# New step times for two list-scheduled stages, a pause step before the page scatters, and the further pages' lists built in pieces

## The chip, the cores and the metric

One core of one Trainium2 chip runs the whole program in one launch. The core has a matrix engine (PE, TensorE), a vector engine (DVE), a scalar engine (ACT), a general engine (POOL, GpSimd) and a sync engine (SP), each with its own queue of instructions that it works off in order; transfers go through DMA queues that SP and POOL fill. The metric is the device time of one execution in microseconds (us); less is better.

## The reference

The input x has 4 batches of 256 tokens with 256 numbers each. Four sublayers follow one another, each as `x = x + layernorm(sublayer(layernorm(x)))`:

```python
# 1 attention over chunks of 32 tokens: 16 query heads, 4 key heads, 128 numbers a head
scores = einsum("bld,bcd->blc", qr, lmk) / sqrt(32)      # token against chunk landmarks
rw  = softmax(scores of the chunks that lie before the token)
att = softmax(q @ k over the 32 tokens of each chunk) * rw[chunk]
out = (att @ v) @ w_o.T + residual

# 2 mixture of experts: 32 experts, each token goes to its best 4
top, idx = top_k(x @ gate_w.T + gate_b, 4); w = softmax(top)
for the rows of one expert:
    gate = minimum(x @ w_gate + b_gate, 7); up = clip(x @ w_up + b_up, -7, 7)
    y = ((up + 1) * gate * sigmoid(1.702 * gate)) @ w_down + b_down
out = sum of the 4 y of a token, weighted by w

# 3 gated scan along the tokens
lam = sigmoid(x @ W.T + b);  s = lam * s + (1 - lam) * x

# 4 gated network with int8 weights, 1024 inner units
out = ((silu((x @ w_gate) * s_gate) * ((x @ w_up) * s_up)) @ w_down) * s_down
```

The 1024 tokens make 8 tiles of 128 tokens, two to a batch. 1024 tokens times 4 choices are 4096 rows for the experts.

## The kernel before

**The planner.** Two stages, attention with routing and the last layer (sublayers 3 and 4), are not written in the order in which they run. Their code is cut into steps, and `Plan` (L49 to L109) decides the order. A step has an engine letter (T is PE, V DVE, A ACT, P POOL, S SP, J a step of no time that only gives buffers back, others are arrivals of data), a cost in us, a list of steps that it comes after, buffers that it takes and gives, and a lead. `run` works backwards first: a step's rank is its lead or, if longer, the longest chain of costs behind it, with a fixed HOP of 0.12 us between two steps. Then it plays the engines forward in pretended time: each engine that is free takes the ready step of the highest rank whose buffers are free, and its code is written out then. So costs and hops do not run on the chip; they set the order in which the code of the steps is emitted. The dependencies on the chip are made from the tiles that the code touches. The framework that builds the program decides the order of the transfers and instructions of each engine again from there, so what runs may differ from the order of the text.

**Attention (the `aplan`, L311 to L997).** `batch(b)` (L572) adds the steps of one batch: statistics and a transposed copy of x, landmark scores and the chunk weights (`hidden`, `shares`, `spread`, `place`, `copy_rw`), keys and values (`keys`, `turn_k`, `values`), queries for each of four key heads (`queries` L821 with four matmuls of 128x512 named pq, `square_sums` L764 named jq, `norm_q` through `power` L336 on POOL named rq, `scale_q` named qn, `turn_q` named pqT), then for each key head the softmax over three pieces of scores: `stage1` on DVE, `less` on POOL (L874), `exps` on ACT, `sums` on DVE, `times` on POOL, `back` on DVE, and `weigh` on PE. The projection (`project` L968, matmuls wo of 128x256, eight to a step) makes the two tiles of a batch from four key heads each. A batch's steps start with the lead `(B - 1 - b) * LEAD`, with LEAD 22, so that earlier batches go first. Five buffers named att hold the weighed values of a key head, used in a fixed rotation.

**Routing (`routing` L400 to L563)** follows each projected tile: its layernorm (rmva, rve, rrsa), residual, the normed tile xn, which goes to DRAM as xn_dram (L440), the gate's matmul, the choice of four experts (`choose`), each row's rank within its expert (`ranks`, `slots`), the lists of who sits where on the pages (`listed`, `sum_lists` L517), and `places`, which makes rowi (L530), the four row numbers of each token. An expert has pages of 128 rows each. Then four scatters per tile (`scatter_token` L244, an indirect DMA issued by POOL) put the tile's xn rows into x_pages in DRAM. The scatters need the zero fill of x_pages to have landed (`ld_zero`). Tiles 0 to 5 add their four scatters right behind `places`, each behind the one before. Tile 6's scatters are held until tile 7's roots are done; tile 7's are issued in `pages`, behind the gathers of the first pages.

`front_ends` collects the steps that read the attention's input weights and xT. When all of them are through, `middle` (L988) frees that memory and loads the weights of experts 4 to 19 there (SP, the loads at L995).

**The pages (`pages` L1201).** 32 first pages and 16 further ones are worked off in pairs, so pg is 0, 2, and so on up to 46. For each pair: `page_fetch` (L1097) brings the rows, by gathers through POOL for the first 8 pages (L1119, index gi), by SP from x_pages for the others (L1100 first, L1110 further pages); `page_in` transposes them (px, pxT); `page_up` (L1145) multiplies with the gate and up weights (pg L1155), bounds the two halves on DVE (g L1160, u L1162), and makes h; `page_down` transposes h (ph, hT), multiplies (po L1184), and POOL scatters the result o into y_dram (L1191). `pages` fetches four pairs ahead, and calls `hook(pg)` once a pair behind `page_up` and the `page_down` of the pair before.

**The further pages' lists (`more_pages` L1228).** Which expert has more than 128 rows is known only after routing. `hook(0)` calls `more_pages`, which makes all of it at one go: the counts (ptot), how many further pages each expert has (more), their running ends (end, base), for each further page its expert (ex, from a comparison cmp of 128x1024 and a sum) and its place in x_pages (hot, again 128x1024, a product and a sum, place), then exi and placei, which SP reads as values to address weights and rows (`weights` L1087 with the value read L1092, `page_fetch` L1110), sel2, and then the row lists of the further pages: at2 and pq (L1283), slot (L1300, four operations), pick2 (L1307), ent2 (L1316, four), 32 matmuls into plist2 (L1324), and si for the scatters of the results. All of this is DVE work but the matmuls.

**The last layer (L1374 to L1651)** is a second `Plan`: weighting of the y_dram rows (mix), layernorms (lst, rss), gate, scan and the int8 network, with its products in pairs of high and low parts (fh, fl).

## Time and profile before

Three timed runs took 574.9, 576.89 and 577.91 us; the median is 576.89. The profiled execution took 573.4 us itself, and the span that the profile covers is 571.6.

| | profiled execution |
|---|---|
| own time, span | 573.4 us, 571.6 us |
| PE busy | 455.6 us, 80% |
| PE weight load | 308.6 us, 54% |
| DVE busy | 357.1 us, 62% |
| ACT busy | 237.7 us, 42% |
| POOL busy | 309.8 us, 54% |
| mean granted PE clock | 0.919 |
| moved by DMA | 80.68 MB |

A page of the profile begins with the busy time of each engine, its share of the span and its number of instructions. Rows of digits follow, one for each engine, with the busy share in tenths of 40 equal slices of the span; PEclk is the clock that PE was granted. A group line names the source line, engine, operation, result and operands, the count, the busy time and the mean in ns, and behind the second bar the engine's idle time just before such instructions with what ended most of it. The windows view gives the same for chosen stretches of the span: start and end, length, then busy time of PE, PE's weight load, DVE, ACT and POOL with the number of instructions in brackets, PE's clock, the share of time that the DMA engines worked, and GB/s. The timeline view lists instructions in order of time: start, duration, engine, line, operation, result and operands, size, and in square brackets the idle time before with what ended it.

The stages lie at these times: start and first loads 0 to 20 us; attention 20 to 315, of which the zero fill of x_pages shares the transfers until about 127; the last tiles' routing 315 to 341; pages 341 to 452; the landing of the last scatters 452 to 463; the last layer 463 to 571.6.

### The profile page before, as it was taken

The numbers are of one execution on the slowest core, as the hardware profiler recorded it, in microseconds if no ns is written. First come the engines' busy times: TensorE is split into PE (matmuls) and PEld (weight loads), VectorE is DVE, ScalarE is ACT, GpSimd is POOL, SyncE is SP. The second block draws the span as 40 slices with busy tenths as digits, with TensorE's granted clock in tenths as the row PEclk, the third lists the DMA queues.
The fourth block names the chain that finished last, engine by engine and source line by source line (L and its number), as shares of the span: only waits on it lengthen the run. The fifth ranks groups of instructions, "written<-read, shape, count | busy, mean of one in ns | idle before, by whom it ended". The sixth has DMA issues, their size and how long they took to land. (4 is left out here: it accounts for less than half of the span.)

```text
span 571.6 us, 7166 instructions
## 1 busy us (share of the span) xinstructions
PE 455.6 (80%) x1965; PEld 308.6 (54%) x1965; DVE 357.1 (62%) x1096; ACT 237.7 (42%) x760; POOL 309.8 (54%) x434
## 2 busy tenths in 40 slices
PE   1879988997959989948999336899999559689980
PEld 0334545754535735526768224677777347467850
DVE  3359985779736868939785673945644316863442
ACT  3556654244424345433331012234943105675541
POOL 7467674544674645676554473164554516766441
PEclk9999999999979998978999657899999969799996
DMA  8999999930010000010381563323857252000001
GB/s 257 361 387 365 349 349 347 336 129 2 20 55 1 11 10 0 20 55 29 120 303 56 177 246 122 98 92 124 306 208 253 83 200 96 1 1 0 10 29 37
DMA packets 59805, 80.68 MB, mean 141 GB/s; under 512 B 5684, under 2 KB 48682, under 8 KB 59760
## 3 DMA queue, kind: packets, MB, share of 16 engines
q1 hardware_dynamic: 54896, 70.33, 36.4%
q0 software_dynamic: 4576, 9.70, 5.0%
q10 hardware_dynamic: 288, 0.15, 0.2%
q8 instruction: 17, 0.28, 0.2%
q14 instruction: 28, 0.23, 0.1%
HBM read 37.16 MB, written 45.09 MB: 144 GB/s over the span
## 5 line engine op out<-in xcount | busy, mean ns | idle before, releaser
L821 PE MATMUL pq<-w_q,xT 128*128 128x512 f32 x128 | 64.6, 629 | 18.3 <-DVE lists L517 6.4
L968 PE MATMUL wo<-w_o,att 128*128 128x256 f32 x256 | 62.4, 387 | 1.2 <-DVE h L981 1.2
L968 PEld LDWEIGHTS wo<-w_o,att 128*128 128x128 f32 x256 | 48.1, 193 | 13.7 <-issue 5.1
L1191 POOL DMA_INDIRECT y_dram<-o,sia x32 | 32.0, 999 | 43.2 <-ACT o L1188 36.8
L821 PEld LDWEIGHTS pq<-w_q,xT 128*128 128x128 f32 x128 | 24.2, 198 | 41.3 <-issue 21.0
L336 POOL TENSOR_TENSOR rq<-ssq,mhalf 128x4 f32<-128x4 f32 x32 | 32.8, 1025 | 24.6 <-DVE ssq L830 18.4
L764 ACT ACTIVATE jq<-pq 128x128 f32<-128x128 f32 x128 | 33.4, 277 | 27.3 <-PE pq L821 26.4
L244 POOL DMA_INDIRECT x_pages<-rxn,rowi x32 | 31.8, 992 | 20.8 <-issue 7.2
L1155 PE MATMUL pg<-wexp,pxT 128*128 128x256 f32 x128 | 38.7, 418 | 4.0 <-ACT pxT L1142 3.8
L1160 DVE TENSOR_SCALAR g<-pg 128x256 f32<-128x256 f32 x24 | 10.1, 423 | 46.0 <-PE pg L1155 29.2
L836 DVE TENSOR_TENSOR qn<-pq,rq 128x512 f32<-128x512 f32 x32 | 21.7, 679 | 16.5 <-POOL rq L336 16.5
L1155 PEld LDWEIGHTS pg<-wexp,pxT 128*128 128x128 f32 x128 | 24.0, 211 | 10.3 <-ACT pxT L1142 4.0
L1572 POOL TENSOR_TENSOR fl<-f,fh 128x512 fp32r<-128x512 f32 x15 | 19.4, 1291 | 15.6 <-ACT fh L1568 15.6
L1467 PE MATMUL y<-yk,mix 128*128 128x256 f32 x64 | 17.9, 432 | 11.5 <-DMA yk<-y_dram 11.0
L844 PE MATMUL pqT<-ident,qn 128*128 128x128 f32 x128 | 20.7, 283 | 7.9 <-ACT qT L852 7.5
L764 ACT ACTIVATION_READ_ACCUMULATOR jq<-pq 128x1 f32 x128 | 26.6, 208 | 0.0
L1188 ACT COPY o<-po 128x512 f32<-128x512 f32 x24 | 14.1, 585 | 24.9 <-PE po L1184 20.4
L844 PEld LDWEIGHTS pqT<-ident,qn 128*128 128x128 f32 x128 | 15.7, 145 | 16.1 <-ACT qT L852 9.1
L1191 POOL DMA_INDIRECT y_dram<-o,sib x16 | 15.7, 984 | 15.3 <-ACT o L1188 12.6
L852 ACT COPY qT<-pqT 128x512 f32<-128x512 f32 x32 | 18.8, 587 | 8.6 <-PE pqT L844 8.6
L1467 PEld LDWEIGHTS y<-yk,mix 128*128 128x128 f32 x64 | 13.4, 218 | 15.1 <-issue 11.4
L1164 ACT ACTIVATE sg<-g 128x256 f32<-128x256 f32 x24 | 10.0, 417 | 26.4 <-DVE g L1160 24.3
(741 smaller groups left out, 1308.0 us busy)
## 6 DMA issues: line engine op xcount, KB each, us to landing
x_pages<-zeros SPq DMA_DIRECT2D x1, 31744.0 KB
wexp<-in_wcat SPq DMA_DIRECT2D x32, 384.0 KB
wov<-in_wcat SPq DMA_DIRECT2D x16, 384.0 KB
yk<-y_dram SPq DMA_DIRECT2D x8, 512.0 KB
xg<-x_pages SPq DMA_DIRECT2D x12, 256.0 KB
w_q<-in_wqT SPq DMA_DIRECT2D x4, 512.0 KB
w_o<-in_woT SPq DMA_DIRECT2D x2, 1024.0 KB
xg<-x_pages SPq DMA_DIRECT2D x16, 128.0 KB
```

What stands on the lines that cost most here:

```text
L244: nc.gpsimd.indirect_dma_start(out=x_views[i * TOPK + k], out_offset=IndirectOffsetOnAxis(ap=rowi[:, k : k + 1], axis=0), in_=xn, in_offse ...
L336: eng.tensor_tensor(dst, src, mhalf[:p, 0:1].to_broadcast([p, n]), ALU.pow)
L764: nc.scalar.activation(junk[:, 0:HD], src[:, ts(j, HD)], AF.Square, accum_out=dst[:, j : j + 1])
L821: nc.tensor.matmul(ps, keep[f"xT{b}"][:, k, ts(i, P)], wq[:, k, ts(kv, 512)], start=(k == 0), stop=(k == KD - 1))
L836: nc.vector.tensor_tensor(buf(p1, "qn", [P, G, HD], f"qn{n}"), keep[f"pq{n}"].rearrange("p (h d) -> p h d", h=G), rq[:, i, ts(kv, G)].unsq ...
L844: nc.tensor.transpose(ps[:, ts(j, P)], keep[f"qn{n}"][:, j, :], ident)
L852: nc.scalar.copy(keep[f"qT{b}{kv}"][:, :, ts(i, P)], keep[f"pqT{n}"].rearrange("p (h n) -> p h n", h=G))
L968: nc.tensor.matmul(keep[f"wo{b}{i}"][:, 0:D], keep[f"att{b}{kv}"][:, j, ts(i, P)], wo[:, kv * G + j, :], start=(kv == 0 and j == 0), stop= ...
L1155: nc.tensor.matmul(ps[:, j, :], xT[:, j, k, :], ws[j][:, ts(k, 2 * I)], start=False, stop=(k == KD - 1),)
L1191: nc.gpsimd.indirect_dma_start(out=y_views[pg + j], out_offset=IndirectOffsetOnAxis(ap=scl[:, q : q + 1], axis=0), in_=o[:, j, :], in_offs ...
L1467: nc.tensor.matmul(ps, mix[:, i * TOPK + k, :], keep[f"yk{i}"][:, k, :], start=(k == 0), stop=(k == TOPK - 1),)
L1572: eng.tensor_tensor(buf("fl", [P, HALF], f"fl{n}{o}", F32R), keep[f"f{n}{o}"], keep[f"fh{n}{o}"].bitcast(F32), ALU.subtract,)
```

## The change

The planner gets a hop for each engine, and keeps, for a step, the latest of its forerunners' ready times rather than that of the last one to end:

```diff
-    def __init__(self):
+    def __init__(self, hops=None):
+
+        self.hops = hops or {}
...
-                rank[a] = max(rank[a], rank[i] + self.HOP)
+                rank[a] = max(rank[a], rank[i] + hop(self.steps[a][0]))
...
                 for j in then[i]:
                     waits[j] -= 1
+                    when[j] = max(when[j], now + cost + hop(eng))
                     if not waits[j]:
-                        heapq.heappush(events, (now + cost + self.HOP, 1, j))
+                        heapq.heappush(events, (when[j], 1, j))
```

Both plans use it, LEAD is smaller, and some 100 costs are rewritten, nearly all to less. Some of them:

```diff
-        aplan = Plan()
+        aplan = Plan({"T": 0.25, "V": 0.15, "A": 0.18, "P": 0.1, "J": 0.0})
...
-        LEAD = 22.0
+        LEAD = 19.0
...
-            a = add("V", 0.65, [a], stats_a)
+            a = add("V", 0.42, [a], stats_a)
...
-            lg = add("T", 0.8, [xT], logits, take=["mm"])
+            lg = add("T", 0.4, [xT], logits, take=["mm"])
...
-                    qt = add("T", 1.8, [xT, ld_wq[kv], turns.get("q")], queries, take=["mm"])
+                    qt = add("T", 1.73, [xT, ld_wq[kv], turns.get("q")], queries, take=["mm"])
...
-                    a = add("A", 1.9, [qt], lambda i=i, kv=kv, n=n: square_sums(
+                    a = add("A", 1.0, [qt], lambda i=i, kv=kv, n=n: square_sums(
...
-                    a = add("P", 1.05 * cols_ / 448, [a], less)
+                    a = add("P", 0.92 * cols_ / 448, [a], less)
...
-        plan = Plan()
+        plan = Plan({"T": 0.25, "V": 0.15, "A": 0.18, "P": 0.1, "S": 1.3})
...
-            a = plan.add("T", 2.0, ready_u, gate, take=["g"])
+            a = plan.add("T", 1.73, ready_u, gate, take=["g"])
```

In routing, the scatters of tiles 0 to 5 each come behind a step of 2.4 us on a pretended engine W, which emits nothing, and tile 6's `places` has a larger lead:

```diff
-            pl = add("V", 0.85, [sl, xn], places, lead=5.0)
+            pl = add("V", 0.5, [sl, xn], places, lead=12.0 if i == TT - 2 else 5.0)
...
-                    at = aplan.add("P", 1.35, [at, ld_zero, *more], put,
+                    if i < TT - 2:
+
+                        at = aplan.add("W", 2.4, [at, ld_zero])
+                    at = aplan.add("P", 1.3, [at, ld_zero, *more], put,
                                    give=["xn"] if k == TOPK - 1 else [])
```

In attention, `place` and `turn_k` join `front_ends`; the att buffers come from a list that the projection of a batch's second tile fills again; and that projection's step for a key head comes behind the first tile's step for the same head:

```diff
+            front_ends.append(a)
             rws = add("V", 0.1, [a], copy_rw, give=["mm"])
...
-                            keep[f"att{b}{kv}"] = atts[(b * HKV + kv) % NATT]
+                            keep[f"att{b}{kv}"] = atts.pop(0)
...
+            first_tile = []
             for i in range(2):
...
+                        if i == 1:
+                            atts.append(keep[f"att{b}{kv}"])
...
+                    if i == 1:
+
+                        after.append(first_tile[kv])
...
+                    if i == 0:
+                        first_tile.append(a)
```

`more_pages` becomes a generator. The expert and the place of each further page are worked out on 32 partitions, one for each further page, and two small matmuls turn them into rows. It yields between its pieces: after base, after the two matmuls, after sel2, after at2, after pq's sum, ahead of each of the four slot operations, of pick2, of each of the four ent2 operations, and of the 32 matmuls.

```diff
-            cmp = mr.tile([P, E, E], F32, tag="cmp", name="cmp")
...
-            ex = mr.tile([P, E], F32, name="ex")
-            nc.vector.tensor_reduce(ex, cmp, AX.X, ALU.add)
...
-            hot = mr.tile([P, E, E], F32, tag="cmp", name="hot")
...
+            yield
+
+
+            at_q = mr.tile([E, E], F32, name="at_q")
+            exq = mr.tile([E, 2], F32, name="exq")
+            nc.vector.tensor_scalar(at_q, end[:E], pcol[:E], None, ALU.is_le)
+            nc.vector.tensor_reduce(exq[:, 0:1], at_q, AX.X, ALU.add)
+            nc.vector.tensor_scalar(exq[:, 0:1], exq[:, 0:1], E - 1.0, None, ALU.min)
+            nc.vector.tensor_scalar(at_q, iota[:E, 0:E], exq[:, 0:1], None, ALU.is_equal)
+            nc.vector.tensor_tensor(at_q, at_q, base[:E], ALU.mult)
+            nc.vector.tensor_reduce(exq[:, 1:2], at_q, AX.X, ALU.add)
...
+            pr = ps_l.tile([P, 3 * E], F32, tag="l", name="prow")
+            for j in range(2):
+                nc.tensor.matmul(
+                    pr[:NB, ts(j, E)], exq[:, j : j + 1].to_broadcast([E, NB]), ident[:E, 0:E],
+                    start=True, stop=True,
+                )
+            yield
             exi = mr.tile([1, E + 1], I32, name="exi")
-            nc.vector.tensor_copy(exi[:, 0:E], ex[0:1, :])
+            nc.vector.tensor_copy(exi[:, 0:E], pr[0:1, 0:E])
...
-            if pg == 0:
-                more_pages()
+            if pg < 22:
+                for _ in range(2):
+                    next(pieces, None)
+            elif pg == 22:
+                for _ in pieces:
+                    pass
```

So `hook` runs two pieces behind each pair of pages, from pair 0 on.

## The prediction

> **What bounds the kernel now.** I read the page first, then the busy time by stretch, then PE's idle stretches with the queue each points to.
>
> ```profile
> PE 455.6 (80%) x1965; PEld 308.6 (54%) x1965; DVE 357.1 (62%) x1096; ACT 237.7 (42%) x760; POOL 309.8 (54%) x434
> ...
> PE   1879988997959989948999336899999559689980
> ...
> L244 POOL DMA_INDIRECT x_pages<-rxn,rowi x32 | 31.8, 992 | 20.8 <-issue 7.2 <-DVE rowi L530 6.2 <-DVE rrnd L529 5.1
> ```
>
> No engine bounds the whole: PE is busiest, and full in most slices of 14.3 us, but it has holes. Three matter here. The windows put numbers on the two stages that the diff touches most:
>
> ```profile
> 127.00:315.00 188.00, 162.19 (x661) 104.14 (x659) 136.81 (x432) 71.89 (x272) 109.69 (x130) 0.95 0.15 53
> 315.00:341.00 26.00, 7.87 (x36) 4.59 (x36) 19.31 (x85) 1.90 (x6) 13.90 (x21) 0.56 0.67 221
> 341.00:374.00 33.00, 26.22 (x136) 20.42 (x135) 20.01 (x43) 8.73 (x17) 11.09 (x12) 0.78 0.34 108
> 374.00:424.00 50.00, 48.94 (x280) 38.88 (x280) 27.16 (x82) 28.31 (x66) 26.80 (x28) 1.00 0.53 183
> ```
>
> The first column after the stretch is its length, then busy PE, PEld, DVE, ACT, POOL, the granted clock. Attention after the zero fill leaves PE idle 25.8 of 188; the first pages run with PE at 26.2 of 33 and a clock of 0.78, later pages at 48.9 of 50. The **first hole** is in attention, and POOL's order of time shows why:
>
> ```profile
> 152.16 1.00 POOL L336 TENSOR_TENSOR rk<-ssk,mhalf 128x4 f32<-128x4 f32 x1
> 153.36 1.14 POOL L244 DMA_INDIRECT x_pages<-rxn,rowi  x1 [0.20 <-issue]
> ...
> 157.36 0.96 POOL L244 DMA_INDIRECT x_pages<-rxn,rowi  x1 [0.30 <-issue]
> 158.34 0.95 POOL L874 TENSOR_TENSOR e13x<-e13x,mx13x 128x448 f32<-128x448 f32 x1
> ...
> 166.97 1.04 POOL L336 TENSOR_TENSOR rq<-ssq,mhalf 128x4 f32<-128x4 f32 x1 [0.87 <-DVE ssq L830]
> ```
>
> Eight scatters, each 0.96 plus 0.30 before the next, stand in the queue with three softmax steps between them. PE in the same stretch:
>
> ```profile
> 156.65 1.00 PE L667 MATMUL xq<-w_lq,xT 128*128 128x64 f32 x8
> 163.78 3.78 PE L821 MATMUL pq<-w_q,xT 128*128 128x512 f32 x4 [6.13 <-DVE lists L517]
> ...
> 170.32 1.88 PE L821 MATMUL pq<-w_q,xT 128*128 128x512 f32 x4
> ```
>
> PE idles 6.13, and then four matmuls that take 1.88 take 3.78. The same happens at 237 to 252 (idle 3.35 and 4.80). The **second hole** is after 315.16, when the projection ends: rmva is done at 314.57, but rve waits behind a third burst until 316.63; later the gathers of the first pages (from 334.97) stand behind tile 6's four scatters. The **third** is in the first pages, on DVE:
>
> ```profile
> 356.11 0.41 DVE L1160 TENSOR_SCALAR g<-pg 128x256 f32<-128x256 f32 x1
> 356.45 4.61 DVE L1300 TENSOR_TENSOR slot<-iota,rf 128x1024 bf16<-128x1024 f32 x4
> 360.99 1.21 DVE L1307 TENSOR_TENSOR pick<-iota,pq 128x1024 bf16<-128x1024 f32 x1
> 362.12 0.41 DVE L1162 TENSOR_SCALAR u<-pg 128x256 f32<-128x256 f32 x1
> 362.45 3.54 DVE L1316 TENSOR_TENSOR ent<-pick,lab 128x768 bf16<-128x768 bf16 x4
> ```
>
> Between g and u of one page stand 5.7 us of list making. Pages (pg's matmuls) start at 353.34, 362.70, 370.36, and later every 3.83 us.
>
> **The change, part by part.** The sum is made against the profiled execution, 573.4 us with a span of 571.6; the runs' median, 576.89, is 1.0061 times that.
>
> *A, scatters spaced (tiles 0 to 5).* Nothing is removed: 24 scatters stay, 1.26 of POOL each. A pretended engine W holds 2.4 before each, so POOL gets other steps between. What the first two bursts cost PE: 6.13 and 1.90 (3.78 less 1.88); 3.35 and 4.80, and after these 0.51 (pqT 1.11 against 0.60) and 0.78 (two s30x 1.70 against 0.92): 17.5. With spacing a POOL step can still meet one scatter: three steps queued in the first burst (e13x's), five in the second (e23x twice, lrs, e30y, rq), eight times 1.26 is 10.1. So the gain lies between 7.4 and 17.5; nothing in the rows prefers an end, since a step meets a scatter or not by chance, and I take the middle, **12.4**.
>
> DVE is busier where the scatters go. Of 32 scatters the longest took 1.14 against a median of 0.96, so all 24 at the longest would add 4.3 of POOL, hidden while POOL is busy 110 of 188. The Trainium skill speaks against spreading them: SBUF — State Buffer, section "SBUF: two separate sides", says that a DMA issued from GpSimd cannot get its descriptors written while DVE runs a two-port operation, and its next section gives 620 ns alone and 3100 ns overlapped. By that rule 24 scatters would hold POOL some 60 us longer, and the part A would be a loss; the row disagrees, and the sum goes by the row.
>
> *B, the tail.* Tiles 4 and 5 scatter at 306.62 to 316.60 under the projection; spaced at about 3.9 (2.4, 1.3 and hops) the last reach past 320. rve then gets back 2.06 less up to 1.26: take 1.4. But one or two scatters can now meet the four root steps between 316.63 and 323.57, 0 to 5.0, take 1.3. Tile 6's places get a lead of 12 instead of 5: its rank was ready at 326.48, its five small operations take 0.82, and rowi came at 329.48, so they can be 2.2 earlier, and with them four scatters and the gathers behind them; at most 4.7 (gi was ready at 330.28), at least 0. Sum **2.3**, from -3.6 to 6.8.
>
> *C, lists in pieces.* Off DVE: cmp 1.26, its reduction 1.20, hot 1.21 and 1.21, its reduction 1.22, 6.1 in all. New: nine operations on 32 rows (bound by the 128x32 rows at 0.17 to 0.23: 1.5 to 2.1), two matmuls (about 0.2 each by ptot's row) and a PE round trip before exi. The rest (at 1.21, pq 1.22, slot 4.61, pick 1.21, ent 3.54: 11.8) stays, but stands behind the pages' own g, u, h and hT rather than ahead of them. It fits into DVE's idle 339.1 to 348.4 and 351.7 to 355.0 (12.6). Pages 6 and 8 came 9.36 and 7.66 after their forerunners, 3.83 would do: 9.4 of excess. A piece of 1.2 can still stand ahead of a page's step, two such are 2.4; and plist2's 32 matmuls (2.9 of PE), which lay in PE's wait, can fall where PE is full: half, 1.4. So **5.6**, from 0 (the order stays) to 9.4. I leave the copy of page 4 where it is: ACT waits 9.7 for it, until 352.70, and the diff doesn't touch that.
>
> What waits anew: exi waits for the row of matmuls; behind it on DVE are placei, sel2 and the pieces; SP's reads of exi wait for it, and behind these on SP stands page 8's fetch, which waits for the last scatter's landing (353.06) anyway.
>
> *D, costs, hops, ready times, LEAD, first_tile, atts, front_ends.* They only change the order; no instruction comes or goes. The new costs are nearer to the rows: four squares 1.0 instead of 1.9 (four jq from 236.87 to 237.88), eight matmuls of 128x256 1.73 (1.89 for wo x8 with its drain). What could be gained: the other 11.5 of PE's idle time in 127 to 315, and 6.3 in the last layer (3.30, 1.44, 0.74, 0.85). What could be lost: a stall like the first hole, 8.0, at each of three handovers. I take **0**. The middle weights move with the longer front_ends, covered by 40 us: they load at 280 to 300 and are read from 341 on; past that, each us late is a us.
>
> Sum: 12.4 + 2.3 + 5.6 = 20.3, so 553.1, and 1.0061 times that is **556.5**. Its own range, with the ends of A, B and C, is 543 to 573.
>
> **Rivals.** *The bursts stay (17%).* The order on an engine needn't be the order of the text: SP issues WT's load at 315.19, ahead of tile 6's xn_dram at 322.06, though the text has it far behind. If POOL takes a scatter whenever its row is ready, A is 0, and C and the 2.2 of B are left: 565.6, 569.1 as a median. Against it: within the bursts softmax steps do come between.
>
> *SP is blocked (13%).* exi came at 335.47; SP's sixteen reads lasted until 345.5, and page 8's fetch then waited 7.5 for the scatters. If exi comes later than 343, the fetch is late by the rest. Behind page 2's u (362.5) the reads end at 372.5, page 8 starts some 6.6 later than now; C turns into -6.6: 565.3, 568.8. Against it: all that exi needs is there at 332.5, while DVE waits for a gather.
>
> *The new order stalls at the handovers (17%), slower.* Place: where one batch's projection and routing meet the next one's front, now near 85, 150 and 245; LEAD falls from 22 to 19, and the second projection tile waits for the first. Price: 8.0 a stall. It decides from 20.3/8.0, so from three on: 577.2, 580.7; with four 588.8. For it: stalls of 1.3 to 2.4 at 85.6, 125.3, 130.2, 212.7 and 265.3 show how little slack PE has there. Against it: costs nearer to the rows should not make more of them.
>
> **How the numbers follow.** Forecast 46%, the two rivals that are faster 17% and 13%, the slower one 17%, and 7% for mixtures that end within 0.5%, which is about what a measurement can tell from no change. So faster 76%, same 7%, slower 17%. The range reaches from 542, A, B and C near their best, to 582, three stalls: that leaves out the four-stall case and gains in D.
>
> **What would show it.** A: no four L244 in a row before 306, and no PE idle time above 3 us in 140 to 260. B: the first gather less than 3.5 us after gi. C: no slot or ent between g and u of a page, page starts 3.83 apart from page 4 on, SP's L1100 still released by the scatters. D: PE idle in 463 to 560 of the same size. Wrong, if POOL's bursts stand as before, if L1100 waits behind reads of exi, or if PE's idle time in attention is above 40 us from 20 to 315.

## The result, and the profile after

The changed kernel takes 580.45 us (median of 7 runs) against 576.89 for the kernel before beside it: ratio 1.0057, 95% interval 1.0033 to 1.0080. It became 0.6% slower, where 556.5 was forecast. The page of its profiled execution (580.45 us itself, span 578.7), the lines that were shown of before:

```profile
PE 456.6 (79%) x1969; PEld 308.8 (53%) x1969; DVE 348.1 (60%) x1097; ACT 240.0 (41%) x762; POOL 312.2 (54%) x434
...
PE   1869997999985988896996156999998197689980
...
L250 POOL DMA_INDIRECT x_pages<-rxn,rowi x32 | 32.1, 1003 | 11.4 <-issue 7.3
```

Work and instructions are nearly the same. DVE is busy 9.0 us less; e2 below, with the new lists alone, shows that these shed 4.9 of it (352.2). PE has holes of the same size in other places. The windows view, cut at the same events in both kernels (127; the last projection matmul's end; gi's end; the last issue into y_dram; the first matmul of y; the first transpose of z; the end), first before:

```profile
127.00:315.16 188.16, 162.35 (x661) 104.14 (x659) 136.81 (x432) 71.89 (x272) 109.85 (x130) 0.95 0.15 53
315.16:330.28 15.12, 5.42 (x28) 3.52 (x28) 10.61 (x56) 1.16 (x4) 5.45 (x13) 0.60 0.63 194
330.28:455.30 125.02, 103.64 (x560) 79.84 (x558) 69.13 (x190) 47.75 (x103) 61.91 (x64) 0.90 0.50 171
463.52:534.90 71.38, 63.25 (x261) 48.47 (x262) 40.93 (x115) 40.33 (x101) 40.77 (x89) 0.89 0.14 47
534.90:571.60 36.70, 20.87 (x93) 15.43 (x91) 13.20 (x33) 13.10 (x26) 13.05 (x22) 0.85 0.09 30
```

and after:

```profile
127.00:311.67 184.67, 162.71 (x671) 105.71 (x669) 136.37 (x442) 70.20 (x257) 107.25 (x133) 0.95 0.14 50
311.67:333.84 22.17, 3.98 (x26) 2.65 (x25) 11.38 (x62) 1.16 (x4) 13.92 (x19) 0.56 0.58 179
333.84:451.90 118.06, 101.30 (x565) 78.49 (x563) 63.51 (x182) 47.73 (x103) 60.93 (x60) 0.92 0.53 179
461.30:539.80 78.50, 65.13 (x264) 49.01 (x265) 41.58 (x115) 44.11 (x104) 41.55 (x90) 0.89 0.13 43
539.80:578.70 38.90, 22.27 (x89) 15.51 (x87) 12.94 (x32) 12.69 (x25) 12.56 (x22) 0.80 0.09 28
```

The second column of each line is a ledger. Attention ends 3.5 earlier; the tail up to gi is 7.0 longer; the pages are 7.0 shorter; the landing of the last scatters (between the third and fourth lines) is 1.2 longer; the last layer takes 117.4 instead of 108.1, 9.3 more. That makes 7.1 in all, the difference of the spans. The medians lie only 3.6 apart, as the profiled execution of before (573.4) was faster than any of its timed runs; the ledger of two single executions shows where the time went, not to the last microsecond. Read line by line: in attention PE's idle time (length less busy) is 22.0 against 25.8, so the holes did not close; in the tail POOL has 13.9 of work against 5.5, so scatters have moved in there; in the last layer PE and ACT are busy 3.3 and 3.4 us longer with nearly as many instructions, and the rest of its 9.3 is waiting.

### The profile page after: what moved, and what is told of

Same layout as the page of the kernel before. It is cut to its first block, busy times and chain, and to the rows that moved or that the text cites. A ratio compares the mean times of both kernels' runs of the same rounds, so it can differ in the third digit from the quotient of the medians.

```text
span 578.7 us, 7180 instructions
## 1 busy us (share of the span) xinstructions
PE 456.6 (79%) x1969; PEld 308.8 (53%) x1969; DVE 348.1 (60%) x1097; ACT 240.0 (41%) x762; POOL 312.2 (54%) x434
## 4 chain that ended last, share of the span: by engine, by line
PE 33%; POOL 23%; DVE 22%; issue 11%; ACT 5%; DMA 4%; SPq 1%; POOLq 0%; ACTq 0%; DVEq 0%
PE pg L1174 5%; POOL x_pages L250 4%; PE pq L832 4%; PE po L1203 3%; POOL rq L342 2%; PE wo L980 2%; POOL rss L1439 2%; PE g L1575 2%; DMA y_dram<-o,sib 2%; POOL y_dram L1210 2%; PE d L1613 1%; DVE qn L847 1%; DMA w_v<-in_wvT 1%; PE u L1575 1%; POOL xg L1138 1%
## 5 line engine op out<-in xcount | busy, mean ns | idle before, releaser
L980 PE MATMUL wo<-w_o,att 128*128 128x256 f32 x256 | 61.1, 381 | 0.0
L1174 PE MATMUL pg<-wexp,pxT 128*128 128x256 f32 x128 | 36.7, 399 | 0.0
L1601 POOL TENSOR_TENSOR fl<-f,fh 128x512 fp32r<-128x512 f32 x15 | 19.3, 1287 | 16.9 <-ACT fh L1597 16.8
L855 PE MATMUL pqT<-ident,qn 128*128 128x128 f32 x128 | 22.3, 301 | 6.5 <-ACT qT L863 4.3
L855 PEld LDWEIGHTS pqT<-ident,qn 128*128 128x128 f32 x128 | 16.6, 155 | 16.1 <-ACT qT L863 8.2
L1590 DVE SCALAR_TENSOR_TENSOR f<-u,cols,sg 128x512 f32<-128x512 f32 x16 | 12.0, 749 | 21.7 <-PE u L1575 14.8
L1210 POOL DMA_INDIRECT y_dram<-o,sib x16 | 15.7, 984 | 16.7 <-ACT o L1207 14.0
L1438 POOL TENSOR_SCALAR ves<-mvs 128x1 f32<-128x1 f32 x32 | 7.6, 237 | 28.1 <-DVE mvs L1432 28.1
L1496 PEld LDWEIGHTS y<-yk,mix 128*128 128x128 f32 x64 | 12.8, 208 | 16.5 <-issue 12.6
```

Of the source, the lines that this page charges most:

```text
L855: nc.tensor.transpose(ps[:, ts(j, P)], keep[f"qn{n}"][:, j, :], ident)
L980: nc.tensor.matmul(keep[f"wo{b}{i}"][:, 0:D], keep[f"att{b}{kv}"][:, j, ts(i, P)], wo[:, kv * G + j, :], start=(kv == 0 and j == 0), stop= ...
L1174: nc.tensor.matmul(ps[:, j, :], xT[:, j, k, :], ws[j][:, ts(k, 2 * I)], start=False, stop=(k == KD - 1),)
L1210: nc.gpsimd.indirect_dma_start(out=y_views[pg + j], out_offset=IndirectOffsetOnAxis(ap=scl[:, q : q + 1], axis=0), in_=o[:, j, :], in_offs ...
L1496: nc.tensor.matmul(ps, mix[:, i * TOPK + k, :], keep[f"yk{i}"][:, k, :], start=(k == 0), stop=(k == TOPK - 1),)
L1601: eng.tensor_tensor(buf("fl", [P, HALF], f"fl{n}{o}", F32R), keep[f"f{n}{o}"], keep[f"fh{n}{o}"].bitcast(F32), ALU.subtract,)
```

## The experiments

Each ratio is against runs of the kernel before on the same chip. Chips differ: the kernel before itself took 570.5 to 571.0 on those that ran e1 to e15, and 576.5 on the one that ran e16 and e17. The kernels with new parts do not all follow the chip: e17, on the slower one, took 575.38, and e13, on a faster one and with a last layer as long, 577.01. So a ratio holds for its chip; e7, which differs from the changed kernel in one hop setting of the last layer, stands at 1.0172 on a faster chip. The stages of the profiles repeat better: the last layer with its old plan took 106.0 to 108.3 in nine of them, and attention with the new plan ends at 309.7 to 313.6 in nine. So the stages carry the argument, for differences beyond that. In all tables and texts "projection" is the end of the last projection matmul, "layer" the time from the first y to the end of the span.

### Which part costs: the layer, the lists, attention

The first four take the change apart. e1 is the changed kernel with the last layer's code of before; e2 the kernel before with the new `more_pages` and `hook` alone; e4 the kernel before with the last layer's new plan alone; e3 drops the pauses:

```diff
# e1, last layer, and so with each cost of its plan
-        plan = Plan({"T": 0.25, "V": 0.15, "A": 0.18, "P": 0.1, "S": 1.3})
+        plan = Plan()
-            a = plan.add("T", 1.73, ready_u, gate, take=["g"])
+            a = plan.add("T", 2.0, ready_u, gate, take=["g"])
# e3, routing
-                    if i < TT - 2:
-                        at = aplan.add("W", 2.4, [at, ld_zero])
                     at = aplan.add("P", 1.3, [at, ld_zero, *more], put,
```

> The changed kernel with the last layer's plan put back (its costs, and one hop of 0.12). The changed kernel took 578.7 as a span, of which 117.4 from the first mixing matmul (y) to the end; before it was 108.1. Theory order: the new costs and hops gave the last layer a worse order, so this run has about 108 there again and ends near 571 us (1.6% under the changed kernel, about 0.99 of before). Rival position: the layer is longer because of what it meets (PE's clock, transfers from the pages), whatever its plan; then it stays at 115 to 118 and the run at 578 to 580.

> The kernel before with the further pages' lists in pieces, and nothing else. Theory: the lists give 6.9 us between gi and the last issue into y_dram (118.1 against 125.0), and lose 1.2 at the landing behind it, so 571 to 572 us, ratio 0.988 to 0.992. Rival: part of that gain belongs to the longer routing tail of the changed kernel, which let weights and transfers run ahead; then the gain here is below 3.5 and the ratio 0.994 or more.

> The changed kernel without the pause steps W; all else as in the changed kernel. Theory: the pauses moved scatters of tiles 4 and 5 among the four root steps of the last two tiles; without them the stretch from the last projection matmul to gi goes back from 22.0 towards 15, and the run takes 573 to 576 us. Rival: the longer tail comes from the costs and the order of the two last tiles on DVE, not from the pauses; then the stretch stays above 20 and the run at 578 to 582. In attention (ends of the sixth tile's projection at 290.6) the theory that the pauses never took hold expects no change over 2 us; if they did spread the scatters, PE's idle time in 127 to 315 grows by 5 or more.

> The kernel before with the last layer's new plan alone. Theory order: loses what the changed kernel lost there, 9 us: about 586 us, ratio 1.014 to 1.018. Rival position: the loss depends on how the layer is met and is under 3 here: ratio below 1.006.

e5 is the kernel before with the new attention alone (costs, hops, LEAD, pauses and the rest of `aplan`).

> The kernel before with the new attention plan alone (costs, hops, LEAD, pauses, lead of tile 6, the att list), lists in one go and the last layer's old plan. With the last layer's old plan and the lists in pieces it stood at 0.9974 of before, and the pieces alone at 1.0016. Theory A (the new order brings the last projection 3 to 5 us forward, and the longer tail gives 1 back): ratio 0.993 to 0.997. Rival: what it gains is due to the pieces that follow it (the row of exi comes earlier); then alone it is at 0.999 or above.

| run | ratio (95%) | projection | gi | last issue into y_dram | layer |
|---|---|---|---|---|---|
| before, after | 1.0057 (1.0033 to 1.0080) | 315.2, 311.7 | 330.3, 333.8 | 455.3, 451.9 | 108.1, 117.4 |
| e1 layer old | 0.9974 (0.9949 to 1.0000) | 309.7 | 331.9 | 449.6 | 106.5 |
| e2 pieces alone | 1.0016 (0.9995 to 1.0036) | 317.2 | 332.2 | 454.8 | 108.1 |
| e3 no pause | 1.0044 (1.0019 to 1.0070) | 312.0 | 331.3 | 448.0 | 115.4 |
| e4 layer alone | 1.0110 (1.0083 to 1.0137) | 315.4 | 330.5 | 451.8 | 115.9 |
| e5 attention alone | 0.9987 (0.9965 to 1.0009) | 311.4 | 333.5 | 449.8 | 106.6 |

The **last layer** is the loss: its new plan takes 115.4 to 117.4 with either attention in front, its old plan 106.5 to 108.1. The rival of position fell by the layer's length in e1 and e4, though e4's ratio, 1.0110, lies between the two theories. The **pieces** alone are worth nothing that can be told from zero, against the 6.9 that I expected of e2 when I wrote it. **Attention** ends 3 to 6 us earlier than before's 315.2 and its tail is 7 longer; e5's ratio lies between its theory A (up to 0.997) and the rival (from 0.999), and can't be told from 1. The **pauses** do nothing to attention in the kernel as changed: without them projection ends at 312.0 instead of 311.7. In the tail they cost 2.9: that of e3 is 19.3 instead of 22.2, which is neither theory's 15 nor its rival's 20 and more.

### Why the pauses did nothing, and what spacing is worth

The queue order of POOL in the changed kernel, at the first eight scatters:

```profile
167.72 0.94 POOL L885 TENSOR_TENSOR e20x<-e20x,mx20x 128x448 f32<-128x448 f32 x1 [1.97 <-DVE rowi L536]
168.85 1.14 POOL L250 DMA_INDIRECT x_pages<-rxn,rowi  x1 [0.18 <-issue]
170.29 0.99 POOL L250 DMA_INDIRECT x_pages<-rxn,rowi  x1 [0.30 <-issue]
171.31 0.95 POOL L885 TENSOR_TENSOR e20x<-e20x,mx20x 128x448 f32<-128x448 f32 x1
172.42 0.98 POOL L250 DMA_INDIRECT x_pages<-rxn,rowi  x1 [0.17 <-issue]
...
178.78 0.96 POOL L250 DMA_INDIRECT x_pages<-rxn,rowi  x1 [0.30 <-issue]
179.76 1.67 POOL L342 TENSOR_TENSOR lrs<-lms,mhalf 32x8 f32<-32x8 f32 x1
181.89 1.01 POOL L342 TENSOR_TENSOR rq<-ssq,mhalf 128x4 f32<-128x4 f32 x1 [0.47 <-DVE ssq L841]
```

and PE behind it:

```profile
183.68 1.02 PE L727 MATMUL pc<-lmk,qrT 32*128 32x8 f32 x4 [4.71 <-DVE qn L847]
```

Six scatters stand in a row from 172.42 on, and lrs comes behind them. PE's pc (idle 4.7 before it) needs lmk, which DVE makes from lrs, and its wait ends with qn, which DVE makes from the rq behind lrs. The plan had written something else. I counted the POOL steps that the plan wrote between one scatter and the next, and the POOL instructions that stand between them in the trace (the bar parts two batches):

```
written by the plan:  1 2 3 1 0 10 10 | 24 | 4 6 3 2 2 1 1
run on the chip:      0 1 0 0 0  0  0 | 52 | 0 0 0 0 2 0 1
```

The pauses worked on paper: in the plan's time the first eight scatters lie between 141 and 177. Then the framework ordered POOL's queue again and closed them up. To give the order to the chip, each scatter of tiles 0 to 5 was bound in the queue behind the POOL instruction written last before it:

```diff
+                        if i < TT - 2:
+                            queue = nc.cur_bb.bb.instructions
+                            last = next(x for x in reversed(queue) if x.engine == nc.gpsimd.engine)
+                            with tc.issue_after(last):
                                 scatter_token(i, k, keep[f"rowi{i}"], keep[f"rxn{i}"])
# e10, besides
-                    if i < TT - 2:
-                        at = aplan.add("W", 2.4, [at, ld_zero])
# e11, besides
-                    if i < TT - 2:
+                    if i < TT - 4:
                         at = aplan.add("W", 2.4, [at, ld_zero])
```

e8 is e1 with this; e10 is e8 without the pauses; e11 is e8 with pauses for tiles 0 to 3 only; e12 is e8 with the lists at one go; e14 is the kernel before with the binding and nothing else. In e8's trace the second row of the count reads 1 2 3 1 0 10 14 | 25 | 4 6 3 4 2 2 2, so the written order reached the chip.

> The changed kernel with the last layer's old plan, and each scatter of tiles 0 to 5 is bound in POOL's queue behind the POOL step that the plan wrote last before it, so that the spacing reaches the built program. Unbound, this kernel stood at 0.9974. Theory (the spacing never reached the queue, and bursts cost PE time): no four scatters in a row before 300 us, PE's idle time between 127 and 300 falls by 5 or more, the sixth tile's projection ends at 280 to 286 rather than 288.6. The rest of the scatters then lies in the tail among the roots, which costs up to 5. Rival (bursts cost PE little, since what waits for POOL there has slack): projection end within 2 us of 288.6 and a ratio of 0.997 or more.

> The kernel with the scatters bound in POOL's queue as the plan wrote them (it stood at 0.9809), but without the pause steps. Theory spacing: without pauses the plan writes scatters 1.3 to 2.2 apart in place of 4, they hold up softmax steps again, PE's idle time between 127 and 300 goes back from 17 towards 22 and the ratio to 0.988 to 0.996. Rival binding: the binding alone is what matters (a softmax step that the plan wrote ahead of a scatter stays ahead), the pause adds nothing: ratio 0.978 to 0.985.

> As the bound kernel with pauses, but pauses for tiles 0 to 3 only, so that the scatters of tiles 4 and 5 are not spread into the last tiles' routing. Theory tail: the stretch from the last projection matmul to the first gather (15.9 and 5.5 there, 21.4 together) gets shorter by 2 to 4 and the ratio is 0.973 to 0.979. Rival: POOL has the same number of scatters to issue there either way, the sum stays within 1 us and the ratio at 0.978 to 0.984.

> As the bound kernel with pauses (0.9809), with the further pages' lists made at one go as before. Theory hidden: what the lists delay lies ahead of page 8, whose rows wait for the last scatter's landing, and the pieces give back later what they gain (32 matmuls where PE is full): ratio 0.978 to 0.984, no difference. Rival: the pieces are worth the 5.6 forecast: ratio 0.988 to 0.992.

> The kernel before with one thing: the scatters of tiles 0 to 5 are bound in POOL's queue behind the POOL step that the plan wrote last before each. Old costs, no pauses, lists at one go, the last layer as before. Theory binding: the order that the old plan wrote already lets softmax steps past the scatters; holding it gives what the bound kernel with new costs gained in attention, 8 or more us: ratio 0.975 to 0.988. Rival: it takes the new costs or hops for the written order to be good; then 0.992 to 1.0.

| run | ratio (95%) | projection | gi | first gather | layer |
|---|---|---|---|---|---|
| e8 bound, pauses | 0.9809 (0.9778 to 0.9841) | 305.1 | 320.9 | 326.4 | 106.6 |
| e10 bound, no pauses | 0.9694 (0.9634 to 0.9754) | 298.6 | 314.7 | 318.9 | 108.1 |
| e11 bound, pauses to tile 3 | 0.9794 (0.9759 to 0.9829) | 305.7 | 321.9 | 326.1 | 108.3 |
| e12 as e8, lists at one go | 0.9780 (0.9752 to 0.9809) | 307.0 | 322.9 | 328.2 | 106.0 |
| e14 bound, old plan | 0.9931 (0.9901 to 0.9961) | 310.5 | 325.4 | 330.1 | 108.1 |

The same place in POOL's queue in e10, the fastest of all (553.62 us against 571.02):

```profile
171.10 0.95 POOL L888 TENSOR_TENSOR e20x<-e20x,mx20x 128x448 f32<-128x448 f32 x1
172.00 1.66 POOL L342 TENSOR_TENSOR lrs<-lms,mhalf 32x8 f32<-32x8 f32 x1
173.86 1.05 POOL L250 DMA_INDIRECT x_pages<-rxn,rowi  x1 [0.20 <-issue]
175.20 1.04 POOL L342 TENSOR_TENSOR rq<-ssq,mhalf 128x4 f32<-128x4 f32 x1 [0.29 <-DVE ssq L844]
176.44 1.04 POOL L250 DMA_INDIRECT x_pages<-rxn,rowi  x1 [0.20 <-issue]
```

and PE:

```profile
177.02 0.61 PE L730 MATMUL pc<-lmk,qrT 32*128 32x8 f32 x4
```

lrs runs at 172.0 instead of 179.8, pc comes without a wait, and at most three of these eight scatters stand in a row. The windows of e1 (the same kernel unbound, with pauses), then of e10 (two lines), then of e15, which has e10's attention and ran on another chip:

```profile
127.00:309.70 182.70, 160.31 (x669) 104.09 (x667) 135.87 (x441) 70.40 (x257) 107.00 (x132) 0.97 0.15 50
127.00:298.55 171.55, 156.59 (x670) 101.55 (x668) 139.52 (x442) 70.38 (x257) 107.80 (x133) 1.00 0.15 54
298.55:314.74 16.19, 4.27 (x27) 2.82 (x26) 11.66 (x61) 1.15 (x4) 11.48 (x17) 0.63 0.61 185
127.00:301.51 174.51, 160.68 (x673) 104.60 (x671) 140.60 (x444) 70.82 (x262) 108.81 (x134) 0.98 0.15 53
```

Attention ends 11.1 earlier than in e1 (309.7): 7.4 of it is idle time of PE that is gone (15.0 against 22.4), and 3.7 is that the same matmuls are busy for less, with the clock granted at 1.00 instead of 0.97. Only the first part repeats: in e15 attention ends 8.2 earlier than in e1, with 13.8 of idle time, but PE is busy 160.7 at a clock of 0.98. So the theory that bursts cost PE time holds, and its rival of slack fell in e8. But the **pauses harm even when they reach the queue**: e8 ends attention 6.5 later than e10 (3.6 later than e15), against my expectation in e10, where the rival of binding alone was the nearer one and still too careful (0.978 to 0.985; it measured 0.9694). e11 shows that this comes from the pauses of tiles 0 to 3, as its attention is that of e8. That the scatters then run on into the next batch's steps would explain it; I did not test that. e11 (0.9794) and e12 (0.9780) stand beside e8 within the noise, e12 as its theory said. e14's ratio is in its rival's range (0.992 to 1.0): bound to the old plan's order, attention ends 4.7 earlier than before, where 8 or more was the theory. In idle time of PE the binding is worth 5.4 on the old plan (20.4 against 25.8) and 7.4 on the new; so of the 6.4 between 4.7 and 11.1 only 2.0 is idle time; the rest is busy time, which did not repeat.

### The tail

POOL's queue in the changed kernel between the last two tiles' steps:

```profile
313.56 0.96 POOL L250 DMA_INDIRECT x_pages<-rxn,rowi  x1 [0.30 <-issue]
314.56 0.24 POOL L438 TENSOR_SCALAR rve<-rmvc 128x1 f32<-128x1 f32 x1
314.96 1.04 POOL L250 DMA_INDIRECT x_pages<-rxn,rowi  x1 [0.17 <-issue]
316.02 0.60 POOL L342 TENSOR_TENSOR rrsc<-rve,mhalf 128x1 f32<-128x1 f32 x1
...
319.43 0.96 POOL L250 DMA_INDIRECT x_pages<-rxn,rowi  x1 [0.30 <-issue]
320.42 0.24 POOL L418 TENSOR_SCALAR rve<-rmva 128x1 f32<-128x1 f32 x1
320.83 1.04 POOL L250 DMA_INDIRECT x_pages<-rxn,rowi  x1 [0.17 <-issue]
321.90 0.59 POOL L342 TENSOR_TENSOR rrsa<-rve,mhalf 128x1 f32<-128x1 f32 x1
```

The roots meet a scatter four times: rmvc was done at 311.39 and rve starts at 314.56 (3.2), rve ends at 314.80 and rrsc starts at 316.02 (1.2), rmva was done at 317.71 and rve starts at 320.42 (2.7), and 320.66 to 321.90 (1.2): 8.3 in all, with DVE idle for 4.5 and 3.8 meanwhile. In the kernel before, the one such wait behind the projection was 2.1 (rmva 314.57, rve 316.63), so 6.2 of the tail's 7.0 are these waits. They add up, since on DVE the next tile's statistics (st of h, which was there at 312.13) run only behind the normed tile that waits for the first root:

```profile
316.66 0.47 DVE L444 TENSOR_SCALAR rxn<-x_all,rmvc,rrsc 128x256 f32<-128x256 f32 x1 [4.53 <-POOL rrsc L342]
317.06 0.41 DVE L396 BATCH_NORM_STATS2 st<-h 128x6 f32<-128x256 f32 x1
```

What another order on DVE would give was not tested. Part comes back: the scatters are then out of the gathers' way, so the first gather follows gi after 1.0 instead of 4.7. From projection to the first gather it is 23.15 against 19.81, a net loss of 3.3. e11, meant to shorten this stretch by 2 to 4, gave 20.4 against e8's 21.3, as its rival said.

### Why the lists in pieces gave nothing

PE at page 8's transposes, in e8 (pieces):

```profile
342.01 0.60 PE L1180 MATMUL pg<-wexp,pxT 128*128 128x256 f32 x2
347.26 0.57 PE L1165 MATMUL px<-ident,xg 128*128 128x128 f32 x3 [4.65 <-DMA xg<-x_pages]
```

and in e12 (lists at one go):

```profile
341.83 1.03 PE L1180 MATMUL pg<-wexp,pxT 128*128 128x256 f32 x4
348.17 1.09 PE L1165 MATMUL px<-ident,xg 128*128 128x128 f32 x4 [5.31 <-DMA xg<-x_pages]
```

Either way PE waits some 5 us for page 8's rows, which SP can fetch only when the last scatter has landed. What the lists delay, pages 4 and 6, lies ahead of that wait and can use it. And the 32 matmuls of plist2 fell at 369.0 to 371.8 in e8, where PE is full (1.7 us of them), against 354.9 to 357.0 in e12. So the pieces gain 0.8 to 2.1 us up to page 8's g (in e8 against e12, e1 against e5, e2 against e4) and give it back: from gi to the last issue into y_dram they take 1.0 to 1.4 longer in the same three pairs. The ratios are 0.9809 against 0.9780, and 1.0016 alone.

So the shorter pages of the changed kernel (7.0) have other sources. The gathers' place after gi is 3.7. The profile of before has its fifth copy of transposed rows (page 4's pxT) 22.4 after gi; e4, with the same code up to the last layer, has it at 15.7, and its pages take 121.3 instead of 125.0. In e14, with the same code there too, the copy comes at 14.7, but the pages take 124.3, as one scatter took 6.42 (see the end). So the pages of one code vary by 3.7 us between profiled executions, and what I read as a feature of the kernel before, the late copy, was one of that one execution.

### Why the last layer got slower

e6 has the layer's old costs with the new hops, e7 the new costs with the old hop:

```diff
# e6: the costs as in e1, and the hops kept
-            a = plan.add("T", 1.73, ready_u, gate, take=["g"])
+            a = plan.add("T", 2.0, ready_u, gate, take=["g"])
# e7: the costs kept, and
-        plan = Plan({"T": 0.25, "V": 0.15, "A": 0.18, "P": 0.1, "S": 1.3})
+        plan = Plan()
```

> The changed kernel; in the last layer's plan only the hops are new (T 0.25, V 0.15, A 0.18, P 0.1, S 1.3), its costs are those of before. Theory costs (smaller costs put the first tiles' high-part transposes vt and the first up-products ahead of the last batch's gate, where PE waits for them): here the layer is as before, 106 to 109 us from the first y to the end, ratio 0.995 to 0.999. Theory hops: the layer stays at 114 to 117, ratio 1.003 to 1.008.

> The changed kernel; in the last layer's plan only the costs are new, the hop is 0.12 for all as before. Theory costs: the layer stays long, 114 to 118 us, ratio 1.003 to 1.009. Theory hops: the layer is back at 106 to 109 and the ratio at 0.995 to 0.999.

e6: ratio 1.0078 (1.0048 to 1.0108), layer 112.2. e7: 1.0172 (1.0144 to 1.0200), layer 117.0. The costs alone do all of the harm; the hops alone do about half. Neither theory foresaw that both hurt.

What the order looks like is seen on ACT, in the changed kernel:

```profile
494.60 0.58 ACT L1468 ACTIVATE vn<-x_all,shs,rss 128x256 f32<-128x256 f32 x1
...
500.38 0.60 ACT L1468 ACTIVATE vn<-x_all,shs,rss 128x256 f32<-128x256 f32 x1
500.88 0.59 ACT L1468 ACTIVATE un<-x_all,shs,rss 128x256 f32<-128x256 f32 x1
```

and in the kernel before:

```profile
495.49 0.61 ACT L1439 ACTIVATE un<-x_all,shs,rss 128x256 f32<-128x256 f32 x1
...
498.24 0.60 ACT L1439 ACTIVATE vn<-x_all,shs,rss 128x256 f32<-128x256 f32 x1 [0.70 <-POOL shs L1412]
499.38 0.60 ACT L1439 ACTIVATE vn<-x_all,shs,rss 128x256 f32<-128x256 f32 x1 [0.55 <-POOL shs L1412]
```

un is the last tile's input of the gate, vn the first tiles' inputs of the network. Before, un comes first, 8.7 after the tile's y; after, it comes behind four vn, 16.6 after its y, and the last batch's gate ends 45.3 after the first y instead of 37.6. Two kernels put it first again, e9 on ACT and PE only, e13 by rank on all engines (for the last two tiles and the last gate):

```diff
# e9
+        for v in turned_v[:4]:
+            plan.steps[v][2].append(last_gate)
+            plan.steps[v - 1][2].append(last_u - 1)
# e13, in Plan.run, with plan.first holding those steps
+        for i in self.first:
+            rank[i] += 1000.0
```

> The changed kernel, new costs and hops in the last layer too; two orders are fixed there: the first four tiles' normed inputs of the network (vn, on ACT) come behind the last tile's normed input of the gate (un), and their transposes (vt, on PE) behind the last batch's gate. Theory chain: in the changed kernel the last tile took 16.6 us from the end of its y to its un, against 8.7 before, because its steps stood behind those of the first four tiles; that is the loss. Then the layer falls from 117.4 to 107 to 111 and the ratio to 0.996 to 1.003. Rival: the loss is in the network's own order (g, u, d with other costs), then the layer stays at 114 or more and the ratio above 1.006.

> The changed kernel, new costs and hops in the last layer; there the steps of the last two tiles from y to the gate's input, and the last gate, get the highest rank on every engine (the run before fixed only ACT's and PE's order: the last tile's way from y to ut fell from 18.1 to 12.8, but the layer stayed at 115.9, because the first tiles then waited too). Theory chain: with its place on DVE and POOL too, that way is 9 to 11 us as in the kernel before (9.4), and the layer takes 106 to 111; ratio 0.994 to 1.003. Rival: it stays above 114 whatever this chain does, and the ratio above 1.007; the loss is then in the order of the network's products.

e9: 1.0125 (1.0097 to 1.0154), layer 115.9, as its rival said. The last tile's way to the start of ut fell from 17.4 to 12.8 (9.4 before), and the first tiles then waited for it. e13: 1.0120 (1.0099 to 1.0142), layer 113.2; that lies between the chain theory's 106 to 111 and its rival's 114. Its way to ut is 10.1, as the theory had it, so that chain is not the whole loss. e15 put e13's layer behind e10's attention, and gave 112.2 there against 108.1, again between theory and rival, with the ratio on the rival's side (0.9827, 0.9795 to 0.9860):

> Bound scatters without pauses (0.9694 with the last layer's old plan), and the last layer with new costs and hops and the last two tiles' steps first. Theory chain: the layer takes 105 to 109 as with the old plan (108.0 there), ratio 0.964 to 0.975. Rival: the new layer stays at 114 or more: ratio 0.978 or more.

The rest lies behind z. From the first transpose of z to the end, all runs with the new costs of the network's steps take 37.3 to 38.9, and those with the old ones 34.3 to 34.6 (the profile of before alone has 36.7). e16 is e13 with the old costs of the network's steps, from the first product on; e17 has the old costs and hop up to there and the new costs behind:

```diff
# e16: e13, and so with each cost from the first product on
-                        "T", 0.92, ready_v[n * TH : (n + 1) * TH] + [last, before.get((tag, o % 2))], up, take=[tag]
+                        "T", 0.94, ready_v[n * TH : (n + 1) * TH] + [last, before.get((tag, o % 2))], up, take=[tag]
# e17: the changed kernel, with each cost ahead of it as before, and
+        plan = Plan()
```

> As the changed kernel with the last two tiles' steps first (layer 113.2, of which 75.9 to the first transpose of z and 37.3 from there), and the costs of the network's steps (products, silu, high, low, z and what follows) as before. Theory two parts: from z on the layer takes 34 to 35 as with the old costs, and the whole 109 to 111; ratio 1.003 to 1.009. Rival one part: from z on it stays at 37 or more, the layer at 112 to 115, ratio 1.009 to 1.015.

> The changed kernel; in the last layer the old costs up to the network's input and the one hop of 0.12, new costs from the network's first product on. Theory two parts: up to z 71 to 75 as before, from z on 37 to 38, the layer 109 to 112; ratio 1.0 to 1.007. Rival front alone: the layer is back at 106 to 108.5, ratio 0.995 to 1.0.

e16: layer 109.1, 34.3 of it from z on; e17: layer 113.6, 37.3 from z on. Both fit two parts in the stage behind z; e17's layer is 1.6 above its range. Their ratios, 0.9921 (0.9893 to 0.9948) and 0.9979 (0.9948 to 1.0010), are from the chip where the kernel before is slower, and lie below what was expected. In time itself e16 is 4.6 under e13 (572.39 against 577.01), much as the layers say. So of the layer's 9.3, the last two tiles' place is 4.2 (117.4 to 113.2), the costs of the network's steps 4.1 (113.2 to 109.1), and 1 is left. These are differences of single profiles on different chips, and a layer of one code varies by some 2 us. Which of those costs does it, and why the slightly shorter ones order the products worse, stays open.

## Why the prediction was wrong

**A, 12.4: the premise failed.** The step that failed is "A pretended engine W holds 2.4 before each, so POOL gets other steps between". It does in the plan and not in the queue. The rival "the bursts stay" named the reason (an engine's order needn't be the text's) and got 17%; the softmax steps seen within the old bursts, held against it, were no evidence. Where the spacing was made to reach the queue (e8), attention gained 4.6 over the same kernel unbound, under A's range of 7.4 to 17.5. Bound without pauses it gained 11.1 (8.2 in e15), inside that range, but 3.7 of the 11.1 is busy time that A did not price. So the mechanism, bursts that cost PE time, was right, and the pause was the wrong means. The fear that scatters among DVE's work would be slow is one that the prediction took from the Trainium skill (SBUF — State Buffer, section "SBUF: two separate sides", with the two times of the section behind it), and from them it worked out an estimate of 60 us. On average e10 shows nothing of that size: the 32 scatters there take 1069 ns against 992 before. What does hold single scatters up are the lists' operations (last section).

**B, 2.3 with a lower end of -3.6: that lower end.** The stretch to the first gather lost 3.3. The step that was too small is "one or two scatters can now meet the four root steps", 1.3: all four met scatters, at 8.3 in all. Nor did the larger lead bring tile 6's rowi forward: it came at 327.5 against 329.5, but the projection ended 3.5 earlier, so it is 1.5 later behind that.

**C, 5.6: worth 0.** "Pages 6 and 8 came 9.36 and 7.66 after their forerunners, 3.83 would do: 9.4 of excess" priced gaps between pages. They lay ahead of a transfer that PE waits for in any case, a wait which the prediction itself quotes when it says that page 8's fetch waits for the last scatter's landing. The half of plist2 put down as lost (1.4) was 1.7.

**D, 0: the term that decided.** "They only change the order; no instruction comes or goes" is true, and the order cost 9.3 in the last layer, and gave some 4 in attention. "costs nearer to the rows should not make more of them" is the sentence that fell: with costs nearer to the rows the layer is slower in every run. So D, put at nothing though no row said which way it would go, is the step that turned the forecast gain into a loss. The rival "the new order stalls at the handovers" had the right kind of mechanism, on the losing side, but put it into attention, where the new order gained.

Rival "SP is blocked" did not happen: exi came only at 354.0, 20.2 after gi and later than the 343 that the rival named, but page 8's fetch stood ahead of it on SP and was still released by the scatters, at 353.08.

Of the signs named, PE's idle time in attention (35.8 from 20 to 311.7) stayed under the 40 that would have shown A wrong; the row of six scatters showed it.

## What to carry to other kernels

When a planner's order passes through a second scheduler, compare the written order with the queue in the trace before pricing any of it; a cost or a pause in the plan binds nothing, and binding the same order was worth 1.7% here (0.9974 to 0.9809). Truer costs of single steps did not make a better order here: take "it only changes the order" as a term with a sign and a size, by stage, not as 0. A hole in front of a transfer that ends later is free, so price a delay from the wait that ends last behind it.

## What the runs showed of the hardware

From 127 us to the end of attention, the clock granted to PE was 0.94 to 0.97 in kernels with 20 to 27 us of idle time there, 0.97 and 0.98 in e8, e11 and e12 with 17 to 18, and 1.00 in e10 with 15. It does not follow the idle time alone: e15, with e10's attention and the same two longest holes (2.63 and 2.19), was granted 0.98, and nearly the same matmuls (673 against 670) were busy 4.1 longer.

Indirect transfers on POOL can be held up by single DVE operations, which the averages hide. In e14 the last scatter starts among the operations of the lists:

```profile
344.31 4.61 DVE L1312 TENSOR_TENSOR slot<-iota,rf 128x1024 bf16<-128x1024 f32 x4
344.46 6.42 POOL L250 DMA_INDIRECT x_pages<-rxn,rowi  x1 [0.30 <-issue]
348.84 1.21 DVE L1319 TENSOR_TENSOR pick<-iota,pq 128x1024 bf16<-128x1024 f32 x1
```

It ends at 350.88, 0.83 behind pick, and page 8's fetch waits for it. In e10 the one that starts at 330.99 beside a single slot, which ends at 332.07, takes 1.93 and ends 0.85 behind it; in e1 the one at 345.61 takes 1.77, and the distance is 0.85 again. The last scatters meet the lists; in attention none took over 1.33. What keeping them apart would give was not tested.

The kernel before differs by 6 us between chips (570.5 and 576.5), more than the 3.6 that the change cost.
